# A convolution block with attention on one core: row sums reordered, edge clears moved ahead of filter loads, one filter sum held back, own output tiles for the last image

## The chip, the core and the metric

The kernel runs on one core of one Trainium2 chip. All data is fp32. The metric is device time in microseconds (us); lower is better. Engines are named as in the profile: PE is the matrix engine (PEld loads its weights), DVE the vector engine, ACT the scalar engine, POOL the GpSimd engine, SP the sync engine, which here issues only transfers. Each engine works through its own list of instructions in order, so an instruction that waits holds up everything behind it on that engine.

## The reference

`x` has 8 images of 512 channels and 32 x 32 pixels. The block normalises each image in 32 channel groups, runs a small network on it and adds the result to `x`:

```python
t = cbs(x, cv1_w, cv1_bn, 0)                 # 1x1 conv 512->512, batch norm, silu
ys = [t[:, :C], t[:, C:]]                    # C = 256
for i in range(N):                           # N = 2
    yi = ys[-1]
    z = cbs(yi, m_cv1_w[i], m_cv1_bn[i], 1)  # 3x3 conv 256->256
    z = bot_attention(z, m_qkv_w[i], m_rw[i], m_rh[i])   # 4 heads of 64, 1024 positions
    z = silu(bn_eval(conv2d(z, m_cv2_w[i], 0), m_cv2_bn[i]))
    ys.append(yi + z)
return cbs(jnp.concatenate(ys, axis=1), cv2_w, cv2_bn, 0)   # 1x1 conv 1024->512
x = x + (that, of the group-normalised x)
```

## The kernel before

The eight images are taken in four pairs (`p` = 0 to 3). For each pair the kernel runs: the 3x3 convolution of both images, then for each image projection, attention, `m2` (the 1x1 convolution behind the attention); all of that twice (n = 0, 1); then the closing 1x1 convolution `cv2`. The opening convolution `cv1` of the next pair is woven into the attentions of the present one. Many 1x1 convolutions are done with Strassen's seven products (`strassen`, `project_strassen`). Pair 0 is special: its filters and sums must first be made from the raw weights, so its `cv1` and its first projection are direct.

**Filters.** The 3x3 convolution is Winograd's: four outputs from six inputs in each direction, in three groups of rows (i = 2, 0, 1) times three of columns. `make_u` (L400) turns one 128-channel chunk `k` of one half `oc` of a raw 3x3 filter into such a transformed filter `u`. Its rows g0, g1, g2 lie in an "area"; the sums over rows that i = 0 needs are g0+g1+g2 and g0-g1+g2. With `summed=True` the first of them is not computed: `load_row` (L134) loads row 0 and then adds rows 1 and 2 onto it by accumulating transfers, issued from POOL, each of which has to wait until the one before it has landed. L408 then makes the second sum on DVE. The six DVE steps that follow for each i are L428 to L433; the steps of i = 1 begin with L414 to L416. The chunks (n, oc, k) in the order of their making are (0,0,0) and (0,0,1), with sums on DVE, then (0,1,0) and (0,1,1), the first two with loaded sums (tile `taps`), and (1,0,0), (1,0,1), (1,1,0), (1,1,1), whose raw filters are loaded by `load_late` (L1728) into the padded planes `Y2` (tile `ypad`), which are not yet in use then. `load_late` is one load of nine taps and three row loads. The last three of these chunks are made step by step behind the first attention of pair 0.

**Tiles.** `tiles_steps` (L529) makes the transformed inputs `v_in` of the 3x3 convolution on DVE. For each i it needs a tile `w_rows` whose two edge columns are cleared by POOL (L561, L562), before L589 reads them. `third_parts` (L1742) does i = 2 for both images of pair 0, between two steps of the first convolution, and then calls `load_late` for the two chunks (1,0,0) and (1,0,1).

**Attention.** `attention_fast` (L1003) runs in 4 groups of 4 pairs of tiles: PE makes logits (L1026), ACT exponentials (L1030, tile `pt`, 6 buffers), DVE adds them up for the sums (L1044, L1046), PE multiplies with v (L1060) into one PSUM tile, which ACT and DVE empty (L1067, L1068). DVE must have added a `pt` before its buffer is free again.

**The last image.** In the last pair, image 7 has half of its `cv2` products made early (`parts`); `cv2` (L1453) adds the second half from PSUM (L1502, DVE), applies silu (L488, ACT) into a tile `t`, adds the input `x_res` (L1481, DVE) and stores (L1482). `t` has tag `h` with 2 buffers, except for the last quarter (tag `rs`), so a silu waits until the store of two tiles before has landed. The nine inputs `x_res` come from POOL (L1470, tag `t`, 4 buffers), the first stores go out from POOL and the last three from SP. The output is 4 blocks (`oc`) of 128 channels by 1024 pixels; the last block is split into 512, 256 and 256 pixels.

**Order.** The Tile framework's planner sets the order of each engine's instructions: it takes them by priority (the order of the program), as soon as its own timing model thinks them ready and a buffer free. `with tc.issue_after(ins)` adds an order: the instructions of the block that run on the engine of `ins` come behind it in that engine's list; it adds no wait between engines. `ring` (L114) hands out 10 buffers of 4 KB per partition for streamed weights; `NX` is 4. At the start, L1628 to L1639 hold the step in which POOL raises 16 batch-norm variances to the power -1/2 (`scaled`, L1630) and then issues the four accumulating row loads of the chunks (0,1,0) and (0,1,1).

Of the kernel before, what the change touches and what calls it, by code (L numbers as in the profile page):

```python
# [44 lines left out]
F32 = mybir.dt.float32  # L45
I32 = mybir.dt.int32
AF = mybir.ActivationFunctionType
ALU = mybir.AluOpType
# [4 lines left out]
P = 128  # L53
# [8 lines left out]
def kernel(  # L62
# [16 lines left out]
    nc = tc.nc  # L79
    B, C1, HW = x.shape  # L80
    C2 = out.shape[1]
    N, C = m_cv1_w.shape[:2]
    F = m_rw.shape[2]
    NX = C1 // P
    NM = C // P
    NO = C2 // P
    NJ = HW // P
    HALF = 512
# [25 lines left out]
    def ring(shape, name):  # L114
        return const.tile(shape, F32, tag="u", name=name, bufs=RING)
# [16 lines left out]
        return inside(yp)  # L132

    def load_row(n, oc, k, area, r, q=None, **kw):  # L134
        (q or nc.gpsimd).dma_start(
            area[:, 9 * P : 12 * P].rearrange("p (t o) -> p t o", o=P),
            m_cv1_w[n, ts(k, P), 3 * r : 3 * r + 3, ts(oc, P)], **kw
        )
# [261 lines left out]
    def make_u(n, oc, k, area, full=None, new=u_new_late, stores=None, summed=True):  # L400

        raw = area[:, : 9 * P].rearrange("p (r c o) -> p r c o", r=3, c=3)
        mid = area[:, 9 * P : 15 * P].rearrange("p (r c o) -> p r c o", r=2, c=3)
        g0, g1, g2 = (raw[:, r] for r in range(3))
        for i in (2, 0, 1):
            if i == 0:
                if summed:
                    last = stt(mid[:, 1], g1, -2.0, mid[:, 0], ALU.mult, ALU.add)  # L408
                else:
                    tt(mid[:, 1], g0, g2, ALU.add)  # L410
                    tt(mid[:, 0], mid[:, 1], g1, ALU.add)
                    last = tt(mid[:, 1], mid[:, 1], g1, ALU.subtract)
            elif i == 1:
                stt(mid[:, 1], g2, 4.0, g0, ALU.mult, ALU.add)  # L414
                stt(mid[:, 0], g1, 2.0, mid[:, 1], ALU.mult, ALU.add)
                last = stt(mid[:, 1], g1, -2.0, mid[:, 1], ALU.mult, ALU.add)  # L416
            rows = raw[:, 0::2] if i == 2 else mid
            c0, c1, c2 = (rows[:, :, c] for c in range(3))
            if full:
                us = [full[i, cp][:, k] for cp in range(3)]  # L420
            else:
                us = [new() for cp in range(3)]
            (u0, u5), (u1, u2), (u3, u4) = ((u[:, :, 0], u[:, :, 1]) for u in us)
            if i < 2:
                yield last
            nc.scalar.activation(u0, c0, AF.Identity, scale=0.25)
            copied_u[0] = nc.scalar.copy(u5, c2)
            tt(u2, c0, c2, ALU.add)  # L428
            tt(u1, u2, c1, ALU.add)
            yield tt(u2, u2, c1, ALU.subtract)  # L430
            stt(u4, c2, 4.0, c0, ALU.mult, ALU.add)
            stt(u3, c1, 2.0, u4, ALU.mult, ALU.add)
            last = stt(u4, c1, -2.0, u4, ALU.mult, ALU.add)  # L433
            if not full or k == NM - 1:
                for cp in range(3):
                    dst = u_dram[n][oc][i][cp]
                    to = (dst, full[i, cp]) if full else (dst[:, k], us[cp])
                    if stores is None:
                        nc.gpsimd.dma_start(*to)
                    else:  # L440
                        stores.append(to)
            yield last
# [41 lines left out]
    def stages(act, small, ps_big, ps_av, n_pt):  # L484
# [6 lines left out]
            return silued[0]  # L491

        shifted, powered, added_eps, k_added = [None], [None], [None], []
        silu_in, last_product, silued, last_exp, m2_silu, conv_product = [], [None], [None], [None], [None], [None]

        def exp_table():
            with tc.issue_after(silued[0].ins):
# [31 lines left out]
        def tiles_steps(yp, put, is_=(0, 1, 2), ec=None, room=None, ec_at=("rs", 4)):  # L529
# [17 lines left out]
            for i in is_:  # L547
                ba = g = None
                if i == 0:
                    ba = row_tile("w_ba")  # L550
                    last = stt(ba, rows(1, 2), -4.0, rows(3, 2), ALU.mult, ALU.add)
                elif i == 1:
                    for j in range(2):
                        ec[j] = act.tile([P, NT, NM * F], F32, tag=ec_at[0], name="w_ec", bufs=ec_at[1])
                        last = tt(ec[j], rows(3 + j)[:, :, 0], rows(1 + j)[:, :, 0], ALU.subtract)
                else:
                    g = row_tile("w_g")
                    last = tt(g, rows(0, 2, 5), rows(2, 2), ALU.subtract)
                yield last
                e = room("w_rows", [P, 2 * NT * NM, F + 2])  # L560
                nc.gpsimd.memset(e[:, :, 0:1], 0.0)  # L561
                nc.gpsimd.memset(e[:, :, F + 1 : F + 2], 0.0)  # L562
                to = [
                    e.rearrange("p (r t k) w -> p r t k w", r=2, t=NT)[:, r, :, :, 1 : F + 1] for r in range(2)
                ]
                if i == 0:
                    tt(to[0], two(ba[:, :, 1]), two(ba[:, :, 0]), ALU.add)
                    last = tt(to[1], two(ba[:, :, 1]), two(ba[:, :, 0]), ALU.subtract)
                elif i == 1:
                    stt(to[0], two(ec[0]), 2.0, two(ec[1]), ALU.mult, ALU.add)  # L570
                    last = stt(to[1], two(ec[0]), -2.0, two(ec[1]), ALU.mult, ALU.add)
                else:
                    stt(to[0], two(ec[1]), 0.25, two(g[:, :, 0]), ALU.mult, ALU.add)
                    last = stt(to[1], two(ec[0]), -4.0, two(g[:, :, 1]), ALU.mult, ALU.add)
                yield last
                d = room("w_d", [P, 4, 2 * NT * NM * NT])

                def cols(at, step=None):

                    return bass.AP(  # L580
                        tensor=e.tensor, offset=e[:, :, at:].offset,
                        ap=[e.ap[0]] + ([] if step is None else [[step, 2]]) + [e.ap[1], [1, NT]],
                    )

                def d_of(j):
                    return d[:, j : j + 2].rearrange("p j (a s) -> p j a s", s=NT)

                M0, M1, M2, M3 = 0, 3 * NT + 1, 2 * NT + 1, NT + 1
                tt(d_of(0), cols(M2, M3 - M2), cols(M0, M1 - M0), ALU.subtract)  # L589
                yield tt(d_of(2), cols(M0 + 1, M1 - M0), cols(M2, M3 - M2), ALU.subtract)  # L590
                v05, v12, v34 = (put(i, cp) for cp in range(3))
                stt(v05, d[:, 0:2], -4.0, d[:, 2:4], ALU.mult, ALU.add)
                stt(v34[:, 0], d[:, 1], 2.0, d[:, 2], ALU.mult, ALU.add)
                yield stt(v34[:, 1], d[:, 1], -2.0, d[:, 2], ALU.mult, ALU.add)
                ab = act.tile([P, 2, 2 * NT * NM, NT], F32, tag="h", name="w_ab", bufs=2)
                stt(ab[:, 0], cols(M2), -4.0, cols(M0 + 1), ALU.mult, ALU.add)
                stt(ab[:, 1], cols(M1), -4.0, cols(M3), ALU.mult, ALU.add)
                a, b = (ab[:, j].rearrange("p a s -> p (a s)") for j in range(2))
                tt(v12[:, 0], a, b, ALU.add)
                yield tt(v12[:, 1], a, b, ALU.subtract)  # L600
# [852 lines left out]
        def cv2(b, w_of, rhs_of, parts=None):  # L1453
# [12 lines left out]
            def residual():  # L1466
                if len(res) < len(places):
# [2 lines left out]
                    nc.gpsimd.dma_start(t[:, :size], rows_of(x, oc, at, size))  # L1470
                    res.append(t)

            for _ in range(4):
                residual()
            done = 0
# [15 lines left out]
            for oc in range(NO):  # L1491
# [16 lines left out]
                with tc.issue_after(added.ins) if final else nullcontext():  # L1508
                    flush()
                for n, (at, size, src) in enumerate(srcs):  # L1510
                    tag = ("h", "h", "rs")[n] if final else "h"
                    t = act.tile([P, HALF], F32, tag=tag, name="t", bufs=4 if tag == "rs" else 2)[:, :size]
                    silu(from_planes(t), by_slot(src), bn_cv2 + oc)
                    q = nc.sync if final else nc.gpsimd
                    late.append(out_later(t, size, q, rows_of(out, oc, at, size), res[done]))
                    done += 1
                if not parts:
# [109 lines left out]
        begin(Y_ORDER[2], range(NX // 2))  # L1627
    with tc.issue_after(made.ins), tc.issue_after(powered.ins):  # L1628
        nc.vector.tensor_scalar(rstd, bnp[:, :, 3], BN_EPS, None, ALU.add)
        scaled = nc.gpsimd.tensor_tensor(rstd, rstd, mhalf[:, :NBN], ALU.pow)  # L1630
        with tc.issue_after(scaled.ins):
            for r in (1, 2):
                for k in range(NM):
                    load_row(0, 1, k, areas[0, 1, k], r, accum_op=ALU.add)
        for _ in range(4):
            made = next(chunk)
    with tc.issue_after(made.ins):
# [104 lines left out]
    def third_parts(done):  # L1742
        for g in range(G):
            s.tiles_in(Y1[g], putter(vs, g), [2], ecs[g])
        with tc.issue_after(after_norm[0].ins):
            late_taps.extend(load_late(0, k, inside(Y2[k])) for k in range(NM))

    with tc.issue_after(s.silued[0].ins):
# [519 lines left out]
```

## Time and profile before

| | us |
|---|---|
| time, median of 3 runs (lowest to highest) | 2281.31 (2277.72 to 2282.78) |
| profiled execution, its own time | 2278.14 |
| span of the profile | 2276.4 |
| PE busy | 2214.4 (97%) |
| DVE busy | 1744.6 (77%) |
| ACT busy | 1103.5 (48%) |
| POOL busy | 225.7 (10%) |
| mean granted PE clock | 0.993 of full |

Stages of the profiled execution: the opening convolution of pair 0 runs to about 78 us, its first 3x3 convolution from 78 to 133, its first attention from 158 to 231; the last product of the kernel ends at 2261.5. A line of the groups or waits names the engine and the source line of the instruction, its operands as "written<-read", and then times; an idle time is put down to what ended it. Busy PE is not PE at its peak, and 97% is a mean over stages with different limits: the 62 us in which PE is not busy lie mostly in the first 180 us and the last 15.

### The profile page before, as it was taken

How to read it: one execution, taken by the hardware profiler on the slowest of the kernel's cores; microseconds unless marked ns; L12 is line 12 of the kernel's file. 1: busy time of each engine (PE TensorE's matmuls, PEld its weight loads, DVE VectorE, ACT ScalarE, POOL GpSimd, SP SyncE). 2: the span in 40 equal slices, each digit the busy share in tenths (PEclk: the TensorE clock that was granted, in tenths of full speed). 3: DMA queues.
4: the chain of work that ended last, by engine and by line, in shares of the span. 5: the costliest groups of instructions: out<-in, count | busy, mean ns of one | idle time of the engine just before them, and what ended most of it. 6: DMA issues, size and time to landing. Idle time of an engine off the chain costs nothing.

```text
span 2276.4 us, 40540 instructions
## 1 busy us (share of the span) xinstructions
PE 2214.4 (97%) x16338; PEld 1081.6 (48%) x16338; DVE 1744.6 (77%) x2686; ACT 1103.5 (48%) x1367; POOL 225.7 (10%) x425
## 2 busy tenths in 40 slices
PE   7799999999999999999999999999999999999997
PEld 3462437443465443734347443654345733473443
DVE  7868889778758689986857868986794868886742
ACT  7445462545225666356323666455622455345533
POOL 3312210000220000000021000000012000000002
PEclk9899999999999999999999999999999999999998
DMA  8853637321473232612168141542136611251114
GB/s 264 287 165 96 214 128 253 112 69 64 112 224 131 79 121 95 219 52 77 52 152 268 33 160 41 178 127 75 57 77 175 224 49 47 75 193 44 48 32 132
DMA packets 134276, 284.60 MB, mean 125 GB/s; under 512 B 34400, under 2 KB 62028, under 8 KB 133056
## 3 DMA queue, kind: packets, MB, share of 16 engines
q1 hardware_dynamic: 101040, 192.64, 25.9%
q0 software_dynamic: 33040, 89.28, 13.5%
q8 instruction: 131, 2.15, 0.4%
q14 instruction: 65, 0.53, 0.1%
HBM read 213.83 MB, written 68.03 MB: 124 GB/s over the span
## 4 chain that ended last, share of the span: by engine, by line
PE 67%; DVE 18%; issue 7%; DMA 4%; ACT 3%; POOL 1%; SPq 0%; DVEq 0%; POOLq 0%; ACTq 0%
PE av_ps L1060 15%; PE l_ps L1026 14%; PE c L1279 9%; PE c_new L1279 6%; PE ps L515 5%; PE p_ps L908 5%; PE m_ps L1259 4%; PE c_ps L645 3%; DVE acc L1046 2%; PE p_ps L914 2%; PE x_ps L1379 2%; PE s_ps L1077 1%; DMA taps<-in_m_cv_w_dram 1%; DVE c_e L672 1%; DMA ypad<-in_m_cv_w_dram 1%
## 5 line engine op out<-in xcount | busy, mean ns | idle before, releaser
L1030 ACT ACTIVATE pt<-l_ps 128x1024 f32<-128x1024 f32 x512 | 495.4, 1023 | 346.7 <-PE l_ps L1026 315.1
L1046 DVE TENSOR_TENSOR acc<-acc,pt 128x1024 f32<-128x1024 f32 x384 | 469.8, 1223 | 86.0 <-ACT pt L1030 62.6
L1026 PE MATMUL l_ps<-q,kr 64*64 64x512 f32 x4096 | 487.6, 592 | 6.8 <-ACT pt L1030 6.0
L1060 PE MATMUL av_ps<-pt,vT 64*64 64x512 f32 x4096 | 487.3, 593 | 6.3 <-DVE z L1068 6.0
L1026 PEld LDWEIGHTS l_ps<-q,kr 64*64 64x64 f32 x4096 | 157.8, 133 | 277.7 <-issue 250.2
L1060 PEld LDWEIGHTS av_ps<-pt,vT 64*64 64x64 f32 x4096 | 155.2, 133 | 281.5 <-issue 238.5
L645 PEld LDWEIGHTS c_ps<-v_in,u 128*64 128x64 f32 x4320 | 235.7, 137 | 5.3 <-issue 5.3
L645 PE MATMUL c_ps<-v_in,u 128*64 128x128 f32 x4320 | 237.5, 273 | 0.0
L650 ACT COPY c_m<-c_ps 128x512 f32<-128x512 f32 x48 | 28.1, 586 | 185.3 <-PE c_ps L645 114.6
L1259 PE MATMUL m_ps<-z,m_sb 128*128 128x512 f32 x256 | 112.5, 592 | 0.0
L908 PE MATMUL p_ps<-t_z,sq 128*128 128x512 f32 x224 | 106.1, 596 | 1.1 <-DVE t_z L892 1.1
L1044 DVE TENSOR_TENSOR acc<-pt 128x1024 f32<-128x1024 f32 x64 | 78.0, 1219 | 34.0 <-ACT pt L1030 34.0
L488 ACT ACTIVATE t<-m_ps,bh,sh 128x512 f32<-128x512 f32 x64 | 46.3, 774 | 87.1 <-PE m_ps L1259 87.1
L908 PE MATMUL p_ps<-z,sq 128*128 128x512 f32 x168 | 80.7, 605 | 4.5 <-ACT z L488 2.5
L1329 POOL DMA_DIRECT2D c_out<-in_x_dram x56 | 50.4, 972 | 311.2 <-ACT c_out L488 307.1
L1259 PEld LDWEIGHTS m_ps<-z,m_sb 128*128 128x128 f32 x256 | 48.3, 190 | 58.8 <-issue 56.2
L488 ACT ACTIVATE c_out<-cz,bh,sh 128x512 f32<-128x512 f32 x14 | 16.7, 1296 | 90.5 <-DVE cz L1356 90.5
L1132 DVE TENSOR_TENSOR z<-z,rs 128x512 f32<-128x512 f32 x64 | 43.8, 685 | 21.5 <-DMA rs<-r_dram 21.3
L908 PEld LDWEIGHTS p_ps<-t_z,sq 128*128 128x128 f32 x224 | 39.8, 190 | 41.7 <-issue 37.0
L1379 PE MATMUL x_ps<-t_x,sw 128*128 128x512 f32 x128 | 55.9, 592 | 0.0
L488 ACT ACTIVATE z<-z,bh,sh 128x512 f32<-128x512 f32 x64 | 47.6, 804 | 14.7 <-DVE z L697 13.9
L1067 ACT COPY z<-av_ps 128x512 f32<-128x512 f32 x64 | 37.5, 585 | 34.6 <-PE av_ps L1060 34.6
(308 smaller groups left out, 3188.6 us busy)
## 6 DMA issues: line engine op xcount, KB each, us to landing
u<-u SPq DMA_DIRECT2D x135, 512.0 KB
sq<-sq SPq DMA_DIRECT2D x42, 384.0 KB
rs<-r_dram SPq DMA_DIRECT2D x118, 128.0 KB
x<-in_x_dram SPq DMA_DIRECT2D x28, 512.0 KB
r_in<-r SPq DMA_DIRECT2D x28, 512.0 KB
y_in<-y SPq DMA_DIRECT2D x28, 512.0 KB
c_out<-in_x_dram POOLq DMA_DIRECT2D x56, 256.0 KB, 5.3
out_dram<-c_out POOLq DMA_DIRECT2D x56, 256.0 KB, 4.1
```

The source lines that it names most:

```text
L488: silued[0] = nc.scalar.activation(dst, src, AF.Silu, scale=sh[:, k : k + 1], bias=bh[:, k : k + 1])
L515: last_product[0] = nc.tensor.matmul(ps[:, half, :], w_of(k), rhs_of(k, half), start=(k == begin), stop=(k == end))
L645: conv_product[0] = nc.tensor.matmul(to[o], us[cp][:, k, row, c, o], rhs, start=(k == 0), stop=(k == NM - 1),)
L908: nc.tensor.matmul(ps[:, o, :], w[:, o, :], rhs, start=not onto, stop=True, skip_group_check=onto)
L1026: nc.tensor.matmul(ps[kh * HD : (kh + 1) * HD, hd, :], kr[r, c, o : o + HD], q[r, c, ts(half, HALF)], start=True, stop=True,)
L1030: last_exp[0] = exp = nc.scalar.activation(pt, ps, AF.Exp, scale=SCALE)
L1044: return nc.vector.tensor_tensor(accs[g], pt[0], pt[1], ALU.add)
L1046: ins = nc.vector.tensor_tensor(accs[g], accs[g], pt[i], ALU.add)
L1060: nc.tensor.matmul(avs[g][hd * HD : (hd + 1) * HD, kh, :], vT[r, j, o : o + HD], pt[i][r, hd, :], start=(j == 0), stop=(j == NJ - 1),)
L1259: nc.tensor.matmul(pss[half][:, oc, :], m2_sb[:, n, k, ts(oc, P)], ao[:, k, ts(half, HALF)], start=(k == 0), stop=(k == NM - 1),)
L1279: nc.tensor.matmul(ps[:, o, :], w[:, k, ts(o, P)], rhs[part][:, c], start=(k == 0 and not onto), stop=(k == KB - 1), skip_group_check=onto,)
L1379: nc.tensor.matmul(ps[:, o, :], w[:, c, ts(o, P)], rhs[c], start=(c == 0 and not onto), stop=(c == 1), skip_group_check=onto,)
```

## The change

Four edits, in the order of the diff's effect in time:

1. Row sums of the first two chunks. The first accumulating row load (row 1 of chunk (0,1,0)) is issued before the power on POOL, and the power is put behind it; the other three follow in the order row 2 of k = 0, rows 1 and 2 of k = 1.
2. In `make_u`, with loaded sums, L408 is put behind the last DVE step of i = 2 of the same chunk.
3. `third_parts`: the late filter loads are put behind the last edge clear (`cleared`) of the tiles that the same function makes.
4. `cv2` with `parts` (the last image only): the four input blocks are loaded whole by SP into ring buffers, the outputs get four ring buffers of their own, and all stores are issued by SP.

```diff
     def load_row(n, oc, k, area, r, q=None, **kw):
-        (q or nc.gpsimd).dma_start(
+        return (q or nc.gpsimd).dma_start(
...
         for i in (2, 0, 1):
             if i == 0:
                 if summed:
-                    last = stt(mid[:, 1], g1, -2.0, mid[:, 0], ALU.mult, ALU.add)
+                    with tc.issue_after(last.ins):
+                        last = stt(mid[:, 1], g1, -2.0, mid[:, 0], ALU.mult, ALU.add)
...
                 nc.gpsimd.memset(e[:, :, 0:1], 0.0)
-                nc.gpsimd.memset(e[:, :, F + 1 : F + 2], 0.0)
+                cleared[0] = nc.gpsimd.memset(e[:, :, F + 1 : F + 2], 0.0)
...
+            if parts:
+                whole = [ring([P, HW], "x_res") for _ in range(NO)]
+                for oc in range(NO):
+                    nc.sync.dma_start(whole[oc], rows_of(x, oc, 0, HW))
+                res = [whole[oc][:, at : at + size] for oc, at, size in places]
+                ends_of = [ring([P, HW], "t") for _ in range(NO)]
             for _ in range(4):
                 residual()
...
-                    tag = ("h", "h", "rs")[n] if final else "h"
-                    t = act.tile([P, HALF], F32, tag=tag, name="t", bufs=4 if tag == "rs" else 2)[:, :size]
+                    if parts:
+                        t = ends_of[oc][:, at : at + size]
+                    else:
+                        t = act.tile([P, HALF], F32, tag="h", name="t", bufs=2)[:, :size]
                     silu(from_planes(t), by_slot(src), bn_cv2 + oc)
-                    q = nc.sync if final else nc.gpsimd
+                    q = nc.sync if parts else nc.gpsimd
...
         nc.vector.tensor_scalar(rstd, bnp[:, :, 3], BN_EPS, None, ALU.add)
-        scaled = nc.gpsimd.tensor_tensor(rstd, rstd, mhalf[:, :NBN], ALU.pow)
+        begun_sum = load_row(0, 1, 0, areas[0, 1, 0], 1, accum_op=ALU.add)
+        with tc.issue_after(begun_sum.ins):
+            scaled = nc.gpsimd.tensor_tensor(rstd, rstd, mhalf[:, :NBN], ALU.pow)
         with tc.issue_after(scaled.ins):
-            for r in (1, 2):
-                for k in range(NM):
-                    load_row(0, 1, k, areas[0, 1, k], r, accum_op=ALU.add)
+            for k, r in ((0, 2), (1, 1), (1, 2)):
+                load_row(0, 1, k, areas[0, 1, k], r, accum_op=ALU.add)
...
             s.tiles_in(Y1[g], putter(vs, g), [2], ecs[g])
-        with tc.issue_after(after_norm[0].ins):
+        with tc.issue_after(after_norm[0].ins), tc.issue_after(s.cleared[0].ins):
             late_taps.extend(load_late(0, k, inside(Y2[k])) for k in range(NM))
```

With `parts`, `residual()` does nothing after the change, since `res` is full from the start.

## The prediction

> **What bounds the kernel now.** PE is busy 97% of the span, and from 200 us to 2261 no wait of PE exceeds 1.1 us in the list of waits. So a gain must come from the places where PE stands still, and these are the head (before 200 us) and the tail. I read the waits of PE and DVE over the first 200 us, then the order in time of the engine that is waited for, then the last 20 us.
>
> The waits (us in total, times, longest), PE first and then DVE:
>
> ```profile
> PE c_ps L645 <- DVE v_in L599: 12.5, 2, 6.9
> PE l_ps L1026 <- ACT pt L1030: 5.2, 2, 4.5
> ...
> DVE ypad L408 <- DMA ypad<-in_m_cv_w_dram: 11.9, 1, 11.9
> DVE w_d L589 <- POOL w_rows L561: 6.8, 2, 3.5
> DVE taps L408 <- DMA taps<-in_m_cv_w_dram: 5.2, 2, 3.2
> ```
>
> PE waits twice for the convolution's inputs (5.6 us at 78, 6.9 at 110) and once for exponentials (4.5 at 180). Behind each stands a wait of DVE: for the row sums (L408 on `taps`), for the cleared edges (L589), and for a late row sum (L408 on `ypad`). POOL's list in order of time shows why the edges are late:
>
> ```profile
> 94.64 1.30 POOL L135 DMA_DIRECT2D ypad<-in_m_cv_w_dram  x1 [4.49 <-DMA ypad<-in_m_cv_w_dram]
> 95.43 0.68 POOL L561 MEMSET w_rows<- 128x32 f32 x1
> ...
> 104.47 1.25 POOL L135 DMA_DIRECT2D ypad<-in_m_cv_w_dram  x1 [2.31 <-DMA ypad<-in_m_cv_w_dram]
> 105.25 0.64 POOL L561 MEMSET w_rows<- 128x32 f32 x1
> ```
>
> The clears need nothing that is late, but stand behind row loads which wait for the row before. DVE's list shows the third wait and what is behind it:
>
> ```profile
> 168.99 0.56 DVE L408 SCALAR_TENSOR_TENSOR ypad<-ypad 128x384 f32<-128x384 f32 x1 [11.86 <-DMA ypad<-in_m_cv_w_dram]
> 169.46 1.22 DVE L1044 TENSOR_TENSOR acc<-pt 128x1024 f32<-128x1024 f32 x1
> ```
>
> This L408 belongs to chunk (1,1,0), whose last row was issued at 164.83 and landed at 168.9; its first reader is L428 at 223.65, yet the attention's first sum is behind it. The tail, ACT's list:
>
> ```profile
> 2262.60 1.89 ACT L488 ACTIVATE t<-part,bh,sh 128x512 f32<-128x512 f32 x2 [1.99 <-DMA out_dram<-t]
> 2265.59 1.29 ACT L488 ACTIVATE t<-part,bh,sh 128x512 f32<-128x512 f32 x1 [1.10 <-DMA out_dram<-t]
> 2269.22 0.84 ACT L488 ACTIVATE t<-part,bh,sh 128x256 f32<-128x256 f32 x1 [2.34 <-DMA out_dram<-t]
> ```
>
> PE ends at 2261.5; the last three silus wait for stores to free their tile.
>
> **What the skill says.** The Trainium skill, "DMA: Bandwidth & Descriptors", section "SWDGE vs HWDGE vs iDMA": accumulating transfers can be issued from GpSimd only, so the row loads stay in POOL's list. The same page, section "Anatomy of one DMA — SWDGE (gpsimd) path": a wait for a semaphore is made by the issuing sequencer before dispatch, not by the DMA engines. The trace agrees: the clears of 95.43 and 105.25 start only when the loads ahead have been issued. "TensorE: Matmul & The Clock Gate", Part 1: after an idle window of some 3.4 us PE runs at half clock until it has been busy as long. The trace agrees: the 96 matmuls L645 from 110.15 take 7.42 us, as many from 84.63 take 5.46, and the clock granted in the stretch 110 to 118 is 0.74:
>
> ```profile
> 103.30:110.00 6.70, 0.00 (x0) 0.00 (x0) 4.08 (x9) 0.00 (x0) 1.48 (x3) 0.80 0.50 61
> 110.00:118.00 8.00, 7.85 (x108) 7.85 (x110) 7.96 (x17) 0.59 (x1) 0.00 (x0) 0.74 0.24 77
> ```
>
> **The start (edits 1 and 2): 2.0 us.** POOL's four row loads were issued at 26.18 (behind the power, which ran from 23.33), 33.52, 34.32 and 39.36; the waited semaphores show that they are already row 1 and row 2 of k = 0, then rows 1 and 2 of k = 1. Issued at 23.33 (its row 0 landed at 22.5), the first is 2.85 us earlier, and so is the chain: sums at 34.8 (from 37.66) and 42.4 (from 45.26). The power ends near 27.0 rather than 26.2; its reader L1641 runs at 31.67, so this costs nothing while 4.6 us of cover last. The first chunk's earlier sum is also worth nothing: its L408 and three sums would end at 36.8 rather than 39.6, but next on DVE is the norm of image 1 (L726), which waits for PE's mean until 39.55, and the rest of the chunk is ordered behind L736 at 41.72. What counts is the second chunk's L408: it stands at 45.28, after 1.98 us of idling, ahead of L432 at 45.76, and DVE has no gap from there to 85. Held behind that chunk's i = 2 it runs some 7 us later, when its row has long landed; L432 follows L773 at 43.31: 45.76 - 43.31 = 2.45, less 0.48 for L408, which only moves: 2.0. So the row loads are hidden in either order. Bounds: 0, if ACT's place in the order or the stores in front of the clear at 61.5 hold DVE back; 3.1, if L432 and L433 also fill the 0.93 before L773. PE's gap of 5.6 at 78.23 shrinks by the same amount.
>
> **The edges (edit 3): 8.0 us.** Without the waits L589 of the first image runs at 92.9, when L574 ends, rather than 96.14, that of the second at 99.2 rather than 105.92: 6.7 us. The clears now come first; the first one's buffer is free at 91.6 (L686), the second's at 95.8 (L594, 99.05 - 3.25). `v_in` is ready at 103.4 instead of 110.1, and PE is free at 103.24: its gap of 6.9 closes, and the slow clock behind it (7.42 - 5.46 = 2.0) goes with it. Not all of that counts, because DVE is then the slower: from L664 of step 3 to the end of the convolution it has only 0.61 + 0.70 us of idling to give. So 6.7 + 1.3 = 8.0; bounds 6.5 and 8.7 (all of the clock). What is moved: eight POOL transfers, from 86.47 to about 96. They took until 108.2, 21.7 us, so they end at 118. Their first reader is L428 at 143.27, 133 after the gains: 15 us of cover. Behind them on POOL there is nothing until 138.
>
> **The held sum (edit 2): 6.3 us.** The first two exponentials are ready at 162.3, so L1044 can start at 162.5 instead of 169.46. From 169.46 to 199.3 DVE has no gap (the attention's adds and the filter steps), so this stretch moves; I add 0.6 for exponentials that are now later than DVE: L1068 of group 1 ends at 193.0 rather than 199.3. PE from group 0 to group 2 took 199.35 - 162.38 = 37.0 us against 14.5 a group in the next ones; at best it gains 37.0 - 29.0 = 8.0. With DVE as limit: 6.3. Bounds 4 (other filter steps move up) and 7.9. The 0.56 of L408 comes after 203, where DVE idles 0.5 to 1.8 us per pair of tiles: free.
>
> **The tail (edit 4): 5.0 us.** PE's end stays. DVE's list there is L1502 at 2261.59, L1481 at 2262.20, two L1502 until 2263.55, L1481 (third block) until 2264.2; the last L1481 wait for ACT. ACT can start at 2262.3: silus at 2262.3, 2263.4 and 2264.0, ending 2264.8. DVE's last adds then end at 2265.8 rather than 2270.86: 5.1. From there to the end of the span took 5.6 us (issue, 2.4 to landing, 3.0 of closing waits). Five stores are now on SP within 3 us, 1 MB in all; from the rows a store of 256 KB lands in 2.0 us and they follow each other at about 1 us, so the last is late by 0.3 to 1. I take 5.0; bounds 4 and 5.5. Ring: 10 buffers, two with weights until the end, eight for four inputs and four outputs, the last free when product "22" ends at 2234.1; first needed at 2241.7. The inputs (4 x 512 KB) leave POOL, where nothing waits for their place.
>
> **Sum.** 2.0 + 8.0 + 6.3 + 5.0 = 21.3: span 2276.4 to 2255.1, that execution 2278.1 to 2256.8. The median stands 3.2 above it: 2281.3 - 21.3 = **2260.0**. From 200 us to 2234 PE has hardly a gap, so an earlier start is kept.
>
> **Rivals.** *DVE takes it back* (0.19): freed of L408, the planner moves other filter steps into the attention; 19.4 of 20 us are busy between 180 and 200, so PE waits as before. Step 3 falls to 0 and the second only gives 6.5: 13.5 us, 2268. For it: DVE is the chain there. Against: the steps are spread by hooks, and those for which tiles lack can't move. *The tail stays* (0.08): if a ring buffer comes late, outputs wait for weights as they did for stores: 16.3 us, 2265. *Nothing* (0.03): the planner's order already differs from the program's for the row loads; if other stalls take the places of all four, within 0.2% of before (4.6 us, about what a measurement of this kernel can tell). *Slower* (0.03): the four whole-image loads wait in SP's list for ring buffers. One placed ahead of the last scale's transfers (issued 2188.5 and 2189.0, landed 2191.9) blocks them until its product ends; PE needs the scale at 2196.1. A wait for product "s1" (2192.7) lands them 3.6 us later with issue and scale, at 2197.0, and costs 0.9 us; it decides only if the block outlasts 2196.1 + 21.3 + 4.6 - 3.6 = 2218, that is if the load waits for one of the last products (2213 to 2234), which need that scale themselves, so such an order can't run.
>
> **Chances.** Main case 0.67 (2256 to 2267: lower bounds sum to 14.5, upper ones to 25.2), rivals as given. The range of 2252 to 2269 takes in both ends, 2.5 us of scatter between runs, and most of the first two rivals. Faster 0.94, same 0.03, slower 0.03.
>
> **What would show it.** Right: L408 no longer waits for DMA; L589 no longer for POOL; PE's gap at 103 gone and the clock there 1.0; groups of the first attention at about 15 us each; L488 at the end without waits for stores, DVE's last add some 4.3 us behind PE's end. Wrong: PE waits for DVE at the same matmuls, or waits for `ypad` loads near L428 of chunk (1,0,0), or a new wait of SP on PE ahead of a transfer that PE needs.

## The result and the profile after

The changed kernel takes 2259.22 us in the median (2258.10 to 2259.99), the kernel before 2281.23 beside it (2277.72 to 2284.75): 22.0 us less, ratio 0.990 with a 95% interval of 0.989 to 0.9915. The forecast was 2260.0, 21.3 us less, with a range of 2252 to 2269.

The two profiled executions are only 18.3 us apart (2278.14 and 2259.8): that of before was 3.1 us quicker than its median, that of after 0.6 slower. So the two traces show where the time went, but not every term at the size that it has in the median.

The page of the changed kernel, its head:

```profile
span 2258.3 us, 40529 instructions
...
PE 2209.8 (98%) x16338; PEld 1079.4 (48%) x16338; DVE 1745.4 (77%) x2686; ACT 1103.8 (49%) x1367; POOL 217.5 (10%) x410
```

PE has 4.6 us less to do (2214.4 before), although it executes the same matmuls: before, those behind two of its long waits ran at a lower clock (0.74 in the stretch 110 to 118, 0.52 from 182 to 186; both places have 1.00 now). Line numbers are one higher than before up to L1470, then 7 to 10 higher. The waits of the changed kernel up to 200 us (us in total, times, longest), PE first, then DVE:

```profile
PE c_ps L646 <- DVE v_in L600: 6.2, 2, 5.3
...
PE av_ps L1061 <- DVE z L1069: 1.4, 1, 1.4
...
DVE acc L1045 <- ACT pt L1031: 7.0, 2, 5.2
...
DVE taps L409 <- DMA taps<-in_m_cv_w_dram: 1.3, 1, 1.3
DVE u_new L432 <- DMA u<-u_new: 1.0, 1, 1.0
```

The waits for `ypad` (11.9) and `w_rows` (6.8) are gone. PE's wait of 6.9 at 110 us has shrunk to 0.87; that at 78 us (5.6, now 5.3) has hardly changed. A new wait stands in the last line. POOL's list in order of time:

```profile
91.30 0.16 POOL L562 MEMSET w_rows<- 128x32 f32 x1 [5.20 <-DVE c_k L687]
...
95.97 0.16 POOL L562 MEMSET w_rows<- 128x32 f32 x1 [4.46 <-DVE w_ab L598]
...
96.50 1.08 POOL L1739 DMA_DIRECT2D ypad<-in_m_cv_w_dram  x1 [0.30 <-issue]
...
115.52 1.25 POOL L135 DMA_DIRECT2D ypad<-in_m_cv_w_dram  x1 [5.64 <-DMA ypad<-in_m_cv_w_dram]
```

The clears wait for their buffers alone, and the filter loads come behind them. The stretches before and after PE's third turn at the convolution (busy us of PE, PEld, DVE, ACT, POOL with counts; granted clock; DMA share; GB/s):

```profile
96.30:103.20 6.90, 5.53 (x41) 3.03 (x39) 6.80 (x15) 2.70 (x3) 3.68 (x4) 1.00 0.69 208
103.20:111.20 8.00, 8.00 (x146) 8.00 (x148) 7.97 (x17) 0.59 (x1) 3.87 (x3) 1.00 0.90 222
```

PE works in the stretch in which it stood idle, and in the next 8 us 146 matmuls fit where 108 did, at clock 1.00 instead of 0.74. DVE at the first attention:

```profile
153.46 1.23 DVE L1045 TENSOR_TENSOR acc<-pt 128x1024 f32<-128x1024 f32 x1 [5.24 <-ACT pt L1031]
154.79 2.55 DVE L1047 TENSOR_TENSOR acc<-acc,pt 128x1024 f32<-128x1024 f32 x2
```

The first sum now waits for the exponentials that it adds, and for no load. The tail in order of time, DVE, then ACT, then SP's stores:

```profile
2247.46 0.69 DVE L1509 TENSOR_TENSOR part<-ps,part 128x512 f32<-128x512 f32 x1 [4.37 <-PE ps L516]
...
2249.33 1.96 DVE L1488 TENSOR_TENSOR t<-t,x_res 128x512 f32<-128x512 f32 x4
2251.20 0.14 DVE L2181 CAST n_good<-g_ps 1x1 int32<-1x1 f32 x1
...
2248.19 2.50 ACT L489 ACTIVATE t<-part,bh,sh 128x512 f32<-128x512 f32 x3 [3.76 <-DVE part L1509]
...
2248.78 3.21 SPq L1489 DMA_DIRECT2D out_dram<-t  x5
```

The silus wait for no store. DVE's last addition ends at 2251.29, 3.8 us after PE's end (9.3 before); but from there to the end of the span it takes 7.0 us, where it took 5.6.

Matching the 16338 recorded matmuls of both traces one by one gives the gain at each place (places by the time before): 0.4 us at the first convolution's first matmul and 0.9 from 83 us; 8.9 behind the third turn (110 before, 103 now) and still at the attention's logits; 15.6 when group 2 of the attention begins; 14.1 to 14.3 from 817 us to PE's end; 18.2 at the end of the span.

### The profile page after: what moved, and what is told of

Same layout as the page of the kernel before. It is cut to its first block, busy times and chain, and to the rows that moved or that the text cites. A ratio compares the mean times of both kernels' runs of the same rounds, so it can differ in the third digit from the quotient of the medians.

```text
span 2258.3 us, 40529 instructions
## 1 busy us (share of the span) xinstructions
PE 2209.8 (98%) x16338; PEld 1079.4 (48%) x16338; DVE 1745.4 (77%) x2686; ACT 1103.8 (49%) x1367; POOL 217.5 (10%) x410
## 4 chain that ended last, share of the span: by engine, by line
PE 71%; DVE 20%; issue 4%; ACT 2%; DMA 2%; POOL 0%; DVEq 0%; SPq 0%; POOLq 0%; ACTq 0%
PE av_ps L1061 16%; PE l_ps L1027 15%; PE c L1280 9%; PE ps L516 7%; PE c_new L1280 6%; PE p_ps L909 5%; PE m_ps L1260 4%; PE c_ps L646 3%; DVE acc L1047 2%; PE p_ps L915 2%; PE x_ps L1380 2%; DVE c_e L673 1%; PE s_ps L1078 1%; DVE c_t L666 1%; DVE c_t L665 1%
## 5 line engine op out<-in xcount | busy, mean ns | idle before, releaser
L909 PE MATMUL p_ps<-z,sq 128*128 128x512 f32 x168 | 80.7, 605 | 4.6 <-ACT z L489 2.6
L489 ACT ACTIVATE c_out<-cz,bh,sh 128x512 f32<-128x512 f32 x14 | 16.7, 1292 | 89.8 <-DVE cz L1357 89.8
```

Source lines behind the costliest of these rows:

```text
L489: silued[0] = nc.scalar.activation(dst, src, AF.Silu, scale=sh[:, k : k + 1], bias=bh[:, k : k + 1])
L909: nc.tensor.matmul(ps[:, o, :], w[:, o, :], rhs, start=not onto, stop=True, skip_group_check=onto)
```

## The experiments

### Each edit alone

Edit 1, the row load ahead of the power (the kernel before, otherwise unchanged):

```diff
+        begun_sum = load_row(0, 1, 0, areas[0, 1, 0], 1, accum_op=ALU.add)
+        with tc.issue_after(begun_sum.ins):
+            scaled = ...
...
```

> Edit 1 alone (the first accumulating row load ahead of the power). Theory S (steps add up, the start is limited by u_new buffers): the second chunk's L408 still stands ahead of its last i = 2 steps but its row lands some 2 us earlier; what is gained there is lost again at the first wait for a u_new store, as in the changed kernel, where DVE began the first 3x3 convolution's inputs only 0.4 us earlier: 0 to 0.9 us faster. Rival R1 (the prediction's step): 2.0 us faster. The clock gap at 103 and all later waits stay.

Measured: 2279.62 against 2280.01, ratio 0.9999 (0.9990 to 1.0008). Edit 1 alone is worth nothing that can be measured; 2.0 us (0.9991) is just inside the interval, but in the one trace the gain isn't there: L408 of the second chunk ran at 45.24, before at 45.28. Its last row was issued 1.15 us earlier (38.21), but landed no earlier: L408 waited 1.7 us for it.

Edit 2, L408 held:

```diff
-                    last = stt(mid[:, 1], g1, -2.0, mid[:, 0], ALU.mult, ALU.add)
+                    with tc.issue_after(last.ins):
+                        last = stt(mid[:, 1], g1, -2.0, mid[:, 0], ALU.mult, ALU.add)
```

> Edit 2 alone (L408 held behind i = 2). Theory S: first attention 6.3 to 6.7 us earlier from group 2 on, plus 0 to 0.9 at the start, since the second chunk's L408 is out of the way there too: 6.3 to 7.6 us faster. Rival R2 (DVE takes it back): other filter steps fill the place, 0 to 2 us. The changed kernel's trace showed 6.7 between the logits' start and group 2, together with the other edits.

Measured: 2269.85, ratio 0.9961 (0.9947 to 0.9974), that is 8.9 us (5.9 to 12.1). The trace has the parts: 1.2 at the first convolution's start, 1.0 at the attention's logits and 7.7 at its group 2, so 6.65 in the attention itself. Its DVE waits up to 200 us:

```profile
DVE w_d L590 <- POOL w_rows L562: 7.2, 2, 4.1
DVE acc L1045 <- ACT pt L1031: 5.2, 1, 5.2
```

The wait for the clears stands untouched, the wait for `ypad` is gone. So rival R2, that DVE takes the place back with other filter steps, has fallen.

Edit 3, the late loads behind the clears:

```diff
+                cleared[0] = nc.gpsimd.memset(e[:, :, F + 1 : F + 2], 0.0)
...
-        with tc.issue_after(after_norm[0].ins):
+        with tc.issue_after(after_norm[0].ins), tc.issue_after(s.cleared[0].ins):
```

> Edit 3 alone (edge clears ahead of the late loads). Theory S: PE's gap at 103 closes, with the slow clock behind it: 7.5 to 8.5 us faster, kept to the end, because the row load of chunk (1,1,0) moves with DVE, and L408's wait in the first attention stays near 12 us. Rival R3 (that load is bound to its own time): the wait in the first attention grows by what was won, and 1 to 2 us are left. Rival R4 (later loads bind): L428 of chunk (1,0,0) waits for its rows, 3 to 6 us.

Measured: 2270.71, ratio 0.9957 (0.9943 to 0.997), 9.8 us (6.8 to 13.0); in the trace 8.4 behind the third turn and 8.2 at group 2. Its waits up to 200 us, DVE, then PE:

```profile
DVE ypad L408 <- DMA ypad<-in_m_cv_w_dram: 12.1, 1, 12.1
...
PE c_ps L645 <- DVE v_in L599: 6.0, 2, 5.6
PE l_ps L1026 <- ACT pt L1030: 5.2, 2, 4.5
```

L408 waits 12.1 us as it did (11.9), 8.2 us earlier: the row load behind it moved along with DVE. R3 has fallen, and so has R4: no `ypad` load is late for L428. So edits 2 and 3 work independently: by time 8.9 and 9.8 alone.

Edit 4, the tail:

```diff
+                whole = [ring([P, HW], "x_res") for _ in range(NO)]
...
+                        t = ends_of[oc][:, at : at + size]
...
+                    q = nc.sync if parts else nc.gpsimd
```

> Edit 4 alone (last image's inputs and outputs in ring tiles, stores from SP). Theory S: nothing moves before 2230 us, the stretch from PE's end to the end of the span shrinks from 14.9 to 10.9: 3.5 to 4.5 us faster. Rival R5: the tail gains the 5.0 of the prediction when the stages before it are as before. Rival R6: the whole-image loads disturb the last weights, 0 or slower.

Measured: 2276.35, ratio 0.9983 (0.9976 to 0.9990), 3.9 us (2.3 to 5.5). From PE's end to the end of the span it took 10.8 us, as in the changed kernel. This run's trace also warns: its instructions before 2200 us are those of before, yet PE began the first convolution 1.7 us later and ended 4.6 us later than in the profiled execution of before.

By their ratios the four single edits give 0.2 + 8.9 + 9.8 + 3.9 = 22.8 us, together they gave 22.3 by the ratio: they add up within the intervals.

### The start: which edit, and how much

Without edit 1 (the changed kernel with the old order of POOL):

```diff
-        begun_sum = load_row(0, 1, 0, areas[0, 1, 0], 1, accum_op=ALU.add)
-        with tc.issue_after(begun_sum.ins):
-            scaled = ...
+        scaled = ...
...
```

> The changed kernel without edit 1 (edits 2, 3 and 4 alone). Theory T: with L408 held behind i = 2 nothing on DVE waits early for the row sums, so their order is worth nothing: 21 to 23 us faster than before, as the changed kernel (22.0). Rival: edit 1 is worth something once L408 is out of the way, since the row chain then bounds the second chunk: 1 to 2 us less, 20 to 21.

With edit 2 for n = 1 only, so that the start is not held:

```diff
-                    with tc.issue_after(last.ins):
+                    with tc.issue_after(last.ins) if n else nullcontext():
```

> The changed kernel with L408 held for the filters of n = 1 only, so that the second chunk's L408 stands ahead of L432 in the start as before, behind rows that come earlier by edit 1. Theory T: the start's gain comes from edit 2, and is 1 to 3 us in the median, more than the 0.4 to 0.9 between the two profiled executions, since the execution of before was a short one: 19 to 21 us faster than before. Rival: the start is worth 0 to 0.9 us: 21 to 22 us faster.

Measured: 2259.38 (ratio 0.9905, 0.9888 to 0.9922) without edit 1, 2260.06 (0.9909, 0.9892 to 0.9925) without the hold at the start; the changed kernel has 2259.22. In medians, edit 1 is worth 0.2 us in the presence of edit 2, the hold at the start 0.7 to 0.8: both are below what these intervals can tell from nothing. The traces of all runs say more about this place, since only the three kinds of start differ. When PE began the first convolution, and how long DVE waited between 44 and 60 us (us, one execution each; e1 to e4 are the single edits, the others variants of the changed kernel that follow below, "both" the early check with the outputs flushed):

```
rows late, L408 not held:   before 78.2   e3 78.4   e4 79.9   no branch, before 80.7
  wait of L408 for its row         2.0      2.0      3.7                     4.7
row early, L408 not held:   e1 78.2   hold for n = 1 only 77.9
  wait of L408 for its row     1.7                        1.5
L408 held:   e2 77.1  without edit 1 77.4  after 77.8  flush 79.0  POOL stores 78.6
             early check 78.6  both 77.0  no branch, after 76.1
  wait of L432 for a u store   0, 0, 1.0, 1.6, 1.6, 1.6, 0.2, 0
```

The means are 79.3, 78.1 and 77.7. With L408 in the way, the start follows the landing of a row (2.0 us of waiting give 78.2 and 78.4, 3.7 and 4.7 give 79.9 and 80.7); held, it follows for the most part the landing of a `u` store, though executions without that wait still spread from 76.1 to 77.4. In the run with the outputs flushed early, for instance, the wait between 44 and 60 us is

```profile
DVE u_new L432 <- DMA u<-u_new: 1.6, 1, 1.6
```

against this one up to 85 us in the kernel before without its closing branch, both chunks together:

```profile
DVE taps L408 <- DMA taps<-in_m_cv_w_dram: 8.8, 2, 4.7
```

So theory T is right on the kind of gain, but about its size one can only say 1.6 us between means of executions that differ by 2 us among themselves; the pair of profiled executions alone would have said 0.4.

### The tail: why 7.0 us behind the last addition

Two runs changed the stores, the first their order, the second their queue:

```diff
                 final = parts and oc == NO - 1
+                if final:
+                    flush()
```

> The changed kernel with one line more in cv2: the two outputs of the third block are flushed ahead of the last block's sums, so DVE adds and SP stores them while PE works on the last block, not behind L1509, which waits 4.4 us for PE. Theory U (the tail gained 4.0, not 5.0, since 1 MB of stores is issued within 3 us and lands late): the last block's three stores follow only 512 KB; the last addition stays within 0.3 us, the end comes 1 to 2 us earlier: 23 to 24 us faster than before. Rival (closing waits and not the stores set the end): within 0.3 us of the changed kernel's 22.0. Rival (DVE's additions set it): last addition and end both 0.6 to 1.3 us earlier.

```diff
-                    q = nc.sync if parts else nc.gpsimd
+                    q = nc.sync if final else nc.gpsimd
```

> The changed kernel with the stores of the first three blocks issued by POOL, as before the change, and those of the last block by SP. Theory U (the last stores wait for bandwidth behind the others): two queues change nothing, 0 to 0.5 us against the changed kernel, with the same lateness of the last store. Rival V (the five stores follow one another on one queue, and that is what makes the last late): 1 to 1.5 us earlier, 23 us faster than before. Rival W (POOL's own issue takes 0.55 us against 0.33, and its closing drain comes later, 3.1 us before the change): 0.5 to 2 us slower than the changed kernel.

Measured: 2259.47 (0.9904, 0.9887 to 0.9920) with the outputs flushed early, 2260.27 (0.9913, 0.9896 to 0.9929) with POOL's stores: neither helps. In the first, SP had only three stores left at the end, but the issue of the second of them took 1.4 us, so the last came 4.7 us after PE's end instead of 4.1. In the second, the last store was issued at the same distance, 4.1, and the end came 0.5 us later. So neither the queue nor the order of the stores decides here. The second run alone would fit theory U, that the bunched stores land late; the first doesn't, and the runs without branch below give its size.

What the trace shows behind the last addition in the changed kernel: the last packets of the stores have ended by 2253.16, yet SP executes nothing from its branch at 2252.82 until 2256.00. The DMA of these last 6.3 us (busy tenths of the 16 engines and GB/s in 40 slices, then the queues with packets, MB and share):

```profile
DMA  9999998029010000000010000002100000400000
GB/s 364 345 325 338 338 351 273 7 52 156 0 52 0 0 0 0 0 0 0 0 52 0 0 0 0 0 0 52 52 0 0 0 0 0 104 0 0 0 0 0
...
q1 hardware_dynamic: 352, 0.36, 16.7%
q14 instruction: 7, 0.06, 3.2%
q8 instruction: 2, 0.03, 3.0%
```

The stores fill the first seven slices (1.1 us); what follows is sparse, with nine instruction fetches in it. The kernel ends with a test of the sums of exponentials (`n_good`): each engine reads it and branches over a general path. The Trainium skill, "Runtime: NRT & Kernel Launch", section "Instruction fetch mechanics", says that a taken branch whose target is not in the window of pages held forces a fetch by DMA before the engine can go on; it gives no time for it. From the branch to the engine's next instruction it took, in the records of both traces:

```
          before: branch at   next after      after: branch at   next after
PE            2265.30           4.2               2252.28           4.5
POOL          2265.46           0.5               2252.23           0.5
ACT           2269.77           2.6               2252.16           2.5
DVE           2270.73           3.1               2252.29           3.5
SP            2272.24           0.5               2252.82           3.2
```

Before, the five branches were spread over 7 us: PE's lay beneath the waits for stores, ACT's beneath the last additions and stores. After, `n_good` comes from DVE behind its last addition (CAST at 2251.20), so that all five branch within 0.7 us. The other runs show that this is no accident of two executions: from the last addition to the end (the closing) it took 5.6 to 6.2 us in the four with the old tail and the branch, 7.0 in the four with the new one (edit 4 alone, the changed kernel, and it without edit 1 or without the hold at the start). To see what the branch costs, it was taken out of both kernels; the general path for sums out of range is left out of them:

```diff
-    held_all = nc.values_load(n_good[0:1, 0:1])
-    with tc.If(held_all < P):
-        ...
```

This takes away the read of `n_good` and the steps that each engine executes behind the branch as well, so what is measured is the whole test.

> The changed kernel without the closing branch: the general path, which is taken where a sum of exponentials is out of range, is left out, and with it the read of n_good on each engine and the branch over that path. Theory B (the end is set by the fetch of instructions behind the branch, which all five engines now take within 0.7 us of each other, behind the last stores): from PE's last product to the end 8.0 to 8.6 us instead of 10.8, so 2.2 to 2.8 us faster than the changed kernel, 24 to 25 faster than before. Rival U (late landing of the bunched stores): 10.3 to 10.8, at most 0.5 us faster.

> The kernel before without the closing branch and the general path behind it, as in the run above. Theory B: its branches of PE and POOL lay 5 to 7 us ahead of SP's, and SP's took 0.5 us, so little is won: from PE's last product to the end 13.6 to 14.4 us instead of 14.8, 0.4 to 1.2 us faster than before. The difference to the run above is then the 5 to 6 us that the additions and stores come earlier. Rival U: 0 to 0.5, and the same for both kernels.

Then the check was moved ahead of the last image's `cv2`, alone and with the early flush:

```diff
+            ends = const.tile([P, 2], F32, name="ends")
...
+            nc.vector.tensor_copy(n_good, g_ps)
             s.cv2(ib, lambda k: low_w[k // 2 - 2][:, k % 2], rhs_direct, parts)
...
```

> The changed kernel with the check of the sums, from its two reductions to n_good, placed ahead of the last image's cv2 rather than behind it, so that no engine waits for DVE's last addition before it reads n_good and branches. Theory B: PE and POOL fetch while the last additions run; ACT, DVE and SP branch as their own lists end: 0.5 to 2 us faster than the changed kernel, 22.5 to 24 faster than before. Rival U, or a fetch of SP that is as long alone (2.5 us or more): 0 to 0.5 us.

> The changed kernel with the check of the sums placed early and with the third block's outputs flushed ahead of the last block's sums. Theory B with stores in the way of the fetch: 1 to 3 us faster than the changed kernel, 23 to 25 faster than before, and more than the early check alone. Rival: the same as the early check alone, or, if SP's last store is held up as in the flush alone (1.4 us for one issue), 0 to 1 us.

Measured in time: 2257.10 (ratio 0.9904, 0.9889 to 0.9919) after without branch, 2279.00 (0.9990, 0.9983 to 0.9997) before without branch, 2257.93 (0.9903, 0.9888 to 0.9918) with the check early, 2257.92 (0.9910, 0.9897 to 0.9924) with both; the kernel before had 2280.21 beside them. The changed kernel has the ratio 0.9902 (0.989 to 0.9915), so by time none of its three variants is shown to be faster, the one without branch included: its four executions took 2254.58 to 2259.00, and the profiled one is the quickest of them. Its saving rests on the traces. The tails inside each trace are steadier, since the scatter of the start drops out. Measured from PE's end, that is from the start of the first addition of the last block:

```
us from PE's end to            last addition   last store issued   end    last addition to end
before                             9.3              9.4            14.9        5.6
before, no branch                  7.8              7.9            11.1        3.3
after                              3.8              4.1            10.8        7.0
after, no branch                   3.8              4.1             7.4        3.5
after, POOL stores                 3.8              4.1            11.3        7.4
after, flushed early               3.7              4.7            10.6        6.9
after, check early                 3.8              4.1            10.2        6.4
after, check early and flushed     3.7              3.7             9.7        6.0
```

The last addition of the changed kernel without branch, and of the one with both:

```profile
2247.37 1.95 DVE L1488 TENSOR_TENSOR t<-t,x_res 128x512 f32<-128x512 f32 x4
2249.24 0.14 DVE L2181 CAST n_good<-g_ps 1x1 int32<-1x1 f32 x1
```

```profile
2246.57 1.35 DVE L1511 TENSOR_TENSOR part<-ps,part 128x512 f32<-128x512 f32 x3 [2.32 <-PE ps L516]
...
2249.82 0.42 DVE L1488 TENSOR_TENSOR t<-t,x_res 128x256 f32<-128x256 f32 x1 [0.17 <-ACT t L489]
```

Their spans end at 2252.8 and 2256.3. What follows: without the branch the closing takes 3.5 us after and 3.3 before, so in these two traces the new place of the stores costs some 0.2. The test with its branch costs 3.4 after and 2.3 before: the difference of 1.1 and the 0.2 are the 1.4 us by which the closing grew, within rounding. The fetches go with it: without the branch no instruction fetch runs between the last addition and the end, in neither kernel. In this the traces agree with the skill's sentence; how much of the 3.4 is fetch and how much the read of `n_good` and the longer list of steps behind the branch was not taken apart. The theory's own numbers for these runs were too small (2.2 to 2.8 for after, 0.4 to 1.2 for before); the direction and the difference of 1.1 between the two hold. The check early saves 0.6 us and with the flush 1.1 inside the trace. The medians of both are 1.3 us below the changed kernel's, but the kernel before was 1.0 us quicker beside them, too, and by ratio nothing is left: that the early check helps is not shown by time.

## Why the prediction was right

**The bound.** Right: what was won was won before 200 us and in the tail. The third turn and the attention gave what was said of them, the start and the tail less; and nothing between 200 us and PE's end took more than 1.5 us back.

**The start, 2.0 (0 to 3.1).** In the pair of profiled executions 0.4 at PE's first matmul, 0.9 a little later; in the means of all executions 1.6; in medians 0.7 to 0.8 for the hold. PE's wait at 78 us shrank by 0.3, not by 2.0. The working was right as far as it went: L432 (now L433) ran at 43.39, the chunk's i = 1 began 2.4 us earlier, and behind L408 at its new place 1.8 of them were left. What the step missed stands next: output tiles of the chunk wait for stores that POOL issues only from 43 us on, and behind L432's wait of 1.0 us 0.4 of the gain remained. In the other runs that wait was 0 to 1.6. The prediction had stores in the way only as a reason for its lower bound, at another place. "Row loads are hidden in either order" was right: edit 1 is worth nothing measurable.

**The edges, 8.0 (6.5 to 8.7).** Measured 8.0 in the pair, 8.4 to 8.2 in the run alone. DVE's sum came as worked out: its inputs for the third turn were ready 6.95 us earlier, 0.4 of them from the start, so 6.6 by edit 3 (6.7 foretold), and both idle times that it had to give, 0.61 and 0.70, are 0.00 now. Seen from PE the same 8.0 are the gap, which shrank by 6.0 and didn't close (0.87 remains), and the slow clock's full 2.0 (96 matmuls in 5.46 us, 7.42 before). The loads were moved by 10 us at no cost: the last row was issued at 115.5, the first reader (L429) ran at 134.4.

**The held sum, 6.3 (4 to 7.9).** Measured 6.65 in the pair (15.6 less 8.9) and 6.65 alone. The groups 0 and 1 took 30.3 us together, 37.0 before. PE still waits 1.4 us for DVE at group 2: DVE is the limit in that stretch, as worked out.

**The tail, 5.0 (4 to 5.5).** This step was mis-sized too: 4.05 in the pair, 3.9 (2.3 to 5.5) by time alone, which doesn't exclude 5.0. The additions came half a us earlier than said (3.8 us behind PE's end against 4.3 foretold), 5.4 earlier than before. The term "issue, 2.4 to landing, 3.0 of closing waits", taken over from before as 5.6, measured 7.0. The prediction did say that the last store is late by 0.3 to 1, but then took 5.0 where 5.1 less that is 4.1 to 4.8. And the 1.4 us by which that term grew have another reason than the one allowed for: in the main not bunched stores but branches that no longer hide beneath other waits. The old tail varies as well: from PE's end to the end it took 14.9 us in the profiled execution, 15.3, 13.3 and 13.9 in those of the first three single edits.

**What was lost on the way.** The prediction kept an earlier start from 200 us to 2234. In the pair, 1.4 us of 15.6 were lost, 1.1 of them at 802 us, where a DVE step waits for a store of `v_new` and stands ahead of one that PE needs. In order of time, DVE, then PE, first before:

```profile
816.05 0.42 DVE L599 TENSOR_TENSOR v_new<-w_ab 128x256 f32<-128x256 f32 x1 [2.50 <-DMA v<-v_new]
...
817.13 1.16 PE L914 MATMUL p_ps<-sq,t_z 128*128 128x128 f32 x8
```

and after:

```profile
801.76 0.43 DVE L600 TENSOR_TENSOR v_new<-w_ab 128x256 f32<-128x256 f32 x1 [3.57 <-DMA v<-v_new]
...
802.84 1.16 PE L915 MATMUL p_ps<-sq,t_z 128*128 128x128 f32 x8 [1.05 <-DVE u_zv L972]
```

The store landed 1.1 us later in relation to PE. Against the profiled execution of before, the run with the tail alone lost 1.1 us at the same matmul and the kernel before without its branch 0.75, with the instructions of before up to there: so it can come with the execution. The runs with edit 1 or edit 3 alone lost 0.1, the one with edit 2 alone 1.15, and of the eight traces of the changed kernel and its variants seven lost 1.1 to 1.5 and one 0.3. Whether edit 2 makes the loss more likely stays open.

**The sum.** The pair gives 0.9 + 8.0 + 6.65 - 1.4 + 4.05 = 18.2 us, 3 less than the 21.3 foretold for exactly this pair. The median gave 22.0. So the closeness of the median, 0.8 us, is in part luck: the sum was 3 us too large for the execution that it was made on, and the median of before lies 3.1 us above that execution, while the changed kernel's lies 0.6 below its own. Why before has more to lose is only in part seen. Two traces with its instructions began the first convolution 1.7 and 2.5 us later, behind row waits of 3.7 and 4.7 us, which edit 2 takes out of the way. But the changed kernel without the hold at the start is only 0.7 to 0.8 us slower in the median, and without edit 1 only 0.2, so row waits at the start don't explain it all; the rest is open.

**The rivals.** "DVE takes it back" fell by edit 2 alone, "nothing" by the time. "The tail stays" fell: no silu waits for a ring buffer. "Slower", by whole-image loads that block SP: SP did stand behind one of the loads, for 16.7 us from 2179, but the last scale's transfers had gone out before it, and no transfer came late for PE; between 817 us and PE's end the gain stays within 0.3 us.

## What to carry to other kernels

Look behind each long wait of an in-order engine for the work that doesn't need what is waited for: one step of 0.56 us, held back, and edge clears of less than 0.7 us, moved ahead, carried most of the gain. When a chain is shortened, ask which wait was hidden beneath it (here the store of an output tile and the test with its branch at the end), since that is where the next part of the gain goes. And a difference of 2 us between two traces is not a measurement as long as the same instructions differ by as much from one execution to the next.

## What the hardware showed that was not expected

- The test and branch at the end of the program cost 3.4 us of the span when all five engines branched within 0.7 us, 2.3 when they were spread over 7 us (one trace each with and without). In the pair the next instruction of PE, DVE and ACT came 2.5 to 4.5 us behind the branch, POOL's 0.5 in every run, SP's 0.5 before and 3.2 after. With the check early, PE's branch lasted 3.9 us all the same (2240.84 to 2244.76), but matmuls already queued ran on beneath it without a gap.
- With the same instructions up to there, in four traces, PE's first convolution began between 78.2 and 80.7 us, by how long DVE waited for accumulating row loads.
- One issue of a store by SP took 1.4 us, where those of the changed kernel's last image took 0.33 to 0.42, while instruction fetches and the reading of `n_good` ran; why was not settled.
